# Second attention: the diffusion products as one stream over 25 row tiles' periods, and the last tile's normalization on VectorE

## The chip, the cores and the metric

The kernel runs on one core of a Trainium2 chip. The core has five engines that each work through their own list of instructions in order and wait for one another by semaphores: TensorE (PE; its weight loads are shown as PEld), VectorE (DVE), ScalarE (ACT), GpSimd (POOL) and SyncE (SP), which issues the DMAs here. The metric is the device time of one execution in microseconds (us); a time given for a kernel is the median of its runs.

## The reference, cut to what matters

A graph with 3327 nodes and 256 features passes through four layers. Each layer's output is added to its input and normalized. The change lies in the last layer, the fourth, which does two steps of this:

```
R = adj + I;  R = R / R.sum(-1, keepdims=True)
for n in range(2):
    A  = top_p_attention(Xa, W1, W2, W3)   # N x N, row by row, top-p = 0.9
    Xf = R @ Xf                            # diffusion
    Xa = A @ Xa                            # attention
    Z  = Z + Xf @ U1[n].T + Xa @ U2[n].T
h = X + Z
out = (h - mean) / sqrt(var + 1e-5) * ln_g + ln_b
x   = layernorm(x + out)
```

`top_p_attention` takes a softmax of a row's logits, keeps the largest probabilities until their sum reaches 0.9, and normalizes what is kept. The kernel computes the exponentials and finds the smallest kept value by a search; it divides by the kept sum at the end, after the product with the values.

## The kernel before, in words

The rows are cut into nt = 26 tiles of 128. The second attention (L1778 to L1840) is a loop `for i in range(-2, nt + 1)`; one pass of it is called a period here, with the number i. In period i several generators are stepped in turn, so that their instructions stand interleaved:

- `logits` (`scores`, L1141): the 832-column pieces of the logits of tile i + 2, two matmuls each (L1154), copied to `e` by ScalarE.
- `searches` (`search_long`, L1421): the search of tiles i, i + 1 and i + 2, in steps. ScalarE makes six passes over a row of 3328 (L1436, L1441, L1456, L1458, L1474, L1487), GpSimd does the one-column arithmetic between them (most at L1444), VectorE then selects candidates (L1503, L1353), ranks them (L1364, L1366), removes ties (L1532) and masks `e` (L1540; for the last tile in two halves at L1534).
- `values` (`attended`, L1318): tile i - 1. The masked `e` is transposed on TensorE in groups of four blocks (L1327), copied to `wt` by ScalarE (L1139 is the helper's line of these copies), and multiplied by the values G (L1341), 26 products.
- `spread` (`diffused`, L1302, and `aggregated`, L1288): a diffusion tile, 26 products of adjacency blocks with the features (L1296), each 128x128 by 128x256; every product shows as two records of TensorE. The adjacency comes in six loads of up to five blocks (L1294, three buffers), a stored sum `s` in another (L1309); GpSimd prepares `t` (L1306, L1310), and VectorE evacuates the accumulator into `xf` (L1315).
- `result` (`second`, L1583): the end of tile i - 2. VectorE combines value accumulator and `xf` (L1586) and takes statistics (L93, L94); GpSimd takes the power of the variance (`power`, L877, L878), standardizes (L1595), multiplies and adds (L1596, L1597); VectorE takes statistics again, GpSimd the power again and a bias (L1605); ScalarE does the second normalization (L1606), and SP stores the tile (L1608).

The diffusion tile of period i is i + 1 (DL = 1): period -1 does tile 0, period 0 tile 1, and so on to period 24 with tile 25. Periods 25 and 26 have no diffusion. At the end of each period what is left of the diffusion tile is finished (`both(spread)`).

The order of instructions on each engine is made by a scheduler that follows the program's order as priority and starts what is ready in its own estimate. ScalarE's passes and copies of this loop, marked `here` or `in_order`, keep the program's order. Value and diffusion accumulators come from the same three PSUM buffers (`acc`), `xf` has four buffers, `t` has two, which `second` shares.

After the loop the last `result` is run to its end, and `unresolved` (L1611) computes a flag for each tile whose search has to be repeated: a few small VectorE instructions, a one-column matmul (L1627), and a read by every engine (L1914) that decides whether a slow branch runs.

Of the kernel before, what the change touches and what calls it, by code (L numbers as in the profile page):

```python
# [9 lines left out]
F32 = mybir.dt.float32  # L10
# [3 lines left out]
ALU = mybir.AluOpType  # L14
# [4 lines left out]
P = 128  # L19
# [23 lines left out]
DL = 1  # L43
# [7 lines left out]
def gnn_kernel(ctx: ExitStack, tc: tile.TileContext, n: int, a: dict, out: bass.AP):  # L51
    nc = tc.nc
    nt = -(-n // P)
# [5 lines left out]
    small = ctx.enter_context(tc.tile_pool(name="small", bufs=4))  # L59
# [31 lines left out]
    def stats(mv, y, order=lambda x: x):  # L91
        st = small.tile([P, 6], F32, name="bnst")
        order(nc.vector.bn_stats(st, y))  # L93
        nc.vector.bn_aggr(mv, st)  # L94

    def standardize(dst, y, mean, rstd):
        nc.vector.tensor_scalar(dst, y, mean, rstd, op0=ALU.subtract, op1=ALU.mult)
# [79 lines left out]
    with tc.tile_pool(name="l1b", bufs=1) as wpool, tc.tile_pool(name="l1at", bufs=2) as l1at:  # L177
# [3 lines left out]
        with tc.tile_pool(name="l0", bufs=1) as pool, tc.tile_pool(name="l0w", bufs=2) as work, \  # L181
# [11 lines left out]
            for j0 in range(0, nh, J0):  # L193
                m = min(J0, nh - j0)
# [17 lines left out]
            for i in range(nh):  # L212
# [12 lines left out]
                for r in range(2):  # L225
                    it = 2 * i + r
# [13 lines left out]
        with tc.tile_pool(name="l1aw", bufs=1) as cwork, tc.tile_pool(name="l1c", bufs=2) as ch, \  # L240
# [103 lines left out]
            def power(rs, var):  # L344

                gps.tensor_scalar(rs, var, EPS, None, op0=ALU.add)
                gps.tensor_tensor(rs, rs, mhalf[:, :var.shape[1]], op=ALU.pow)
# [128 lines left out]
            shares = {}  # L476
# [264 lines left out]
            for k, (c, s) in enumerate(states):  # L741
                w = us[c].shape[2]
                m = tiles_of(c)
# [59 lines left out]
                if c and 9 <= s < 9 + tiles_of(c - 1):  # L803
                    rs, nb = plus[:2]
                    i = s - 9
                    x = X[:, starts[c - 1] // P + i, :]
# [37 lines left out]
            m = tiles_of(nch - 1)  # L844
            h = prods[k % 2]
# [4 lines left out]
            for i in range(m):  # L850
                it = starts[nch - 1] // P + i
# [16 lines left out]
    with tc.tile_pool(name="l3", bufs=1) as pool, tc.tile_pool(name="l3d", bufs=1, space=DRAM) as dram:  # L868
# [433 lines left out]
        def diffused(work, atp, psum, p, it, out, each=J3):  # L1302

            rd = rdeg[:, it:it + 1]
            t = work.tile([P, D], F32, name="t")
            nc.gpsimd.tensor_scalar(t, (Y if p else X)[:, it, :], rd, None, op0=ALU.mult)  # L1306
            if p:
                s = work.tile([P, D], F32, name="s")
                nc.sync.dma_start(s, sd[it])  # L1309
                nc.gpsimd.tensor_tensor(t, t, s, op=ALU.add)  # L1310
            for acc in aggregated(atp, psum, it, Y if p else X, each):
                if acc is None:
                    yield
            d = work.tile([P, D], F32, name="xf", bufs=DL + 3)
            nc.vector.scalar_tensor_tensor(d, acc, rd, t, op0=ALU.mult, op1=ALU.add)  # L1315
            out.append(d)
# [266 lines left out]
        def second(work, psum, it, acc, f, xf):  # L1583

            h = work.tile([P, D], F32, name="h")
            nc.vector.scalar_tensor_tensor(h, acc, f, xf, op0=ALU.mult, op1=ALU.add)  # L1586
            xb = work.tile([P, D], F32, name="t")
            nc.gpsimd.tensor_tensor(xb, X[:, it, :], b3, op=ALU.add)
            mv = small.tile([P, 2], F32, name="mv")
            stats(mv, h)  # L1590
            rs = small.tile([P, 1], F32, name="rs")
            yield
            with tc.issue_after(edge[0].ins) if edge[0] else nullcontext():
                power(rs, mv)
                nc.gpsimd.tensor_scalar(h, h, mv[:, 0:1], rs, op0=ALU.subtract, op1=ALU.mult)  # L1595
            nc.gpsimd.tensor_tensor(h, h, g3, op=ALU.mult)  # L1596
            nc.gpsimd.tensor_tensor(h, h, xb, op=ALU.add)  # L1597
            yield
            mv = small.tile([P, 2], F32, name="mv")
            stats(mv, h, here)  # L1600
            rs = small.tile([P, 1], F32, name="rs")
            power(rs, mv)
            yield
            nb = small.tile([P, 1], F32, name="nb")
            nc.gpsimd.tensor_scalar(nb, mv[:, 0:1], rs, -1.0, op0=ALU.mult, op1=ALU.mult)  # L1605
            here(nc.scalar.activation(h, h, AF.Identity, scale=rs, bias=nb))  # L1606
            m = min(P, n - it * P)
            nc.sync.dma_start(out[it * P:it * P + m, :], h[:m, :])  # L1608
            yield

        def unresolved(sm, psum, p):  # L1611


            tol = 4e-6
            tot, v, kept = tots[p], vs[p], kepts[p]
            a, f1, f2 = (sm.tile([P, nt], F32, name=x, bufs=1) for x in ("fa", "f1", "f2"))
            nc.vector.scalar_tensor_tensor(a, tot, -TOP_P, kept, op0=ALU.mult, op1=ALU.add)
            nc.vector.scalar_tensor_tensor(f1, tot, tol, a, op0=ALU.mult, op1=ALU.add)

            nc.vector.tensor_scalar(f1, f1, 0.0, None, op0=ALU.is_ge)  # L1620
            nc.vector.tensor_sub(a, a, v)
            nc.vector.scalar_tensor_tensor(f2, tot, -tol, a, op0=ALU.mult, op1=ALU.add)
            nc.vector.scalar_tensor_tensor(f1, f2, 0.0, f1, op0=ALU.is_lt, op1=ALU.mult)
            nc.vector.tensor_scalar(f1, f1, -1.0, 1.0, op0=ALU.mult, op1=ALU.add)
            nc.vector.tensor_mul(f1[:, nt - 1:], f1[:, nt - 1:], valid)
            pf = psum.tile([P, 4, P], F32, name="tp")[:1, 0, :nt]
            nc.tensor.matmul(pf, ones[:, 0:1], f1, start=True, stop=True)  # L1627
            fl = pool.tile([1, nt + 1], F32, name=f"fl{p}")
            nc.vector.tensor_copy(fl[:, :nt], pf)
            nc.vector.reduce_sum(fl[:, nt:], pf, axis=AX.X)  # L1630
            return fl

        def both(*parts):

            parts = list(parts)
            while parts:
                parts = [x for x in parts if next(x, parts) is not parts]

        with tc.tile_pool(name="l3w", bufs=2) as work, tc.tile_pool(name="l3s", bufs=4) as sm:
# [13 lines left out]
            with tc.tile_pool(name="l3p", bufs=2, space=PSUM) as psum, tc.tile_pool(name="l3a", bufs=1) as quads:  # L1653
# [62 lines left out]
                spread = spreading(1)  # L1716
# [61 lines left out]
            with tc.tile_pool(name="l3q", bufs=3, space=PSUM) as psum, tc.tile_pool(name="l3at", bufs=3) as atp, \  # L1778
                    tc.tile_pool(name="l3b", bufs=2) as lone:
                es, searches, xfs = {}, {}, []  # L1780
                result = iter(())
                for i in range(-2, nt + 1):
                    def search(t):
                        if 0 <= t < nt:
                            next(searches[t])

                    values, logits, spread = iter(()), iter(()), iter(())
                    if 0 < i:
                        values = attended(lone, psum, es[i - 1], G, 3, in_order(nc.scalar.copy))
                    if i + 2 < nt:  # L1790
                        logits = start(1, i + 2, es, searches, search_long)
                    more = range(len(xfs), min(nt, i + DL + 1))
                    spread = (x for j in more for x in diffused(lone, atp, psum, 1, j, xfs, 1))

                    def slot(products, looks, pair=False):


                        if pair:
                            next(logits, None)
                        for _ in range(products * len(more)):  # L1800
                            next(spread, None)
                        if pair:
                            next(logits, None)
                        next(values, None)
                        search(looks)

                    search(i)
                    slot(3, i + 1, True)
                    next(result, None)
                    search(i)  # L1810
                    search(i + 1)
                    search(i)
                    next(logits, None)
                    next(result, None)
                    for _ in range(3 * len(more)):
                        next(spread, None)
                    next(logits, None)
                    search(i + 2)
                    next(values, None)
                    search(i)  # L1820
                    next(result, None)
                    slot(3, i + 1, True)
                    slot(3, i + 1, True)
                    for _ in result:
                        pass
                    both(logits)
                    search(i)
                    slot(5, i + 2)
                    search(i + 1)
                    search(i)  # L1830
                    slot(5, i + 1)
                    slot(4, i + 1)
                    both(spread)
                    search(i)
                    if 0 < i:
                        f = normalizer(sm, kepts[1][:, i - 1:i], tots[1][:, i - 1:i])
                        result = second(lone, psum, i - 1, next(values), f, xfs[i - 1])
                both(result)
                edge[0] = None
                fl = unresolved(sm, psum, 1)  # L1840

            fi0 = pool.tile([1, nt + 1], I32, name="fi0")
            fi1 = pool.tile([1, nt + 1], I32, name="fi1")
# [139 lines left out]
```

## Time and profile before

| | |
|---|---|
| median of 3 runs | 3426.72 us (3426.38 to 3440.84) |
| the profiled execution's own time | 3433.03 us |
| its span, first to last instruction | 3431.1 us |
| busy share of the span | PE 92%, PEld 75%, DVE 78%, ACT 51%, POOL 33% |
| mean granted TensorE clock | 0.964 |
| second attention, from the first attention's flags to the end | 2566.6 to 3431.1 us |

The span is what the profiler saw of one execution; the time of that execution is 1.9 us longer. Times in the views count from the span's start. A busy TensorE is not TensorE at its peak, since matmuls overlap and their ends are modelled; the spacing of starts says more than a single duration. In a line of the timeline the bracket gives the idle time of the engine just before and the instruction that ended it.

### The profile page before, as it was taken

The numbers are of one execution on the slowest core, as the hardware profiler recorded it, in microseconds if no ns is written. First come the engines' busy times: TensorE is split into PE (matmuls) and PEld (weight loads), VectorE is DVE, ScalarE is ACT, GpSimd is POOL, SyncE is SP. The second block draws the span as 40 slices with busy tenths as digits, with TensorE's granted clock in tenths as the row PEclk, the third lists the DMA queues.
The fourth block names the chain that finished last, engine by engine and source line by source line (L and its number), as shares of the span: only waits on it lengthen the run. The fifth ranks groups of instructions, "written<-read, shape, count | busy, mean of one in ns | idle before, by whom it ended". The sixth has DMA issues, their size and how long they took to land. (4 is left out here: it accounts for less than half of the span.)

```text
span 3431.1 us, 50276 instructions
## 1 busy us (share of the span) xinstructions
PE 3140.4 (92%) x18301; PEld 2565.8 (75%) x18301; DVE 2686.5 (78%) x5895; ACT 1735.4 (51%) x2764; POOL 1127.6 (33%) x1332
## 2 busy tenths in 40 slices
PE   8999888898988776999989999999998999999996
PEld 5999657676675554888778888888885677777775
DVE  4655368999999997877578778778755898988886
ACT  1000456767767675111133333333337788888883
POOL 0000245666665654111400000000003566656563
PEclk9999999999999988999999999999998999999998
DMA  6775334334343322444322232232213122222220
GB/s 200 251 253 188 105 101 125 110 108 116 102 115 89 69 57 81 150 137 151 115 76 87 65 88 79 69 89 80 71 50 102 52 68 68 64 66 65 72 64 16
DMA packets 206264, 344.31 MB, mean 100 GB/s; under 512 B 22223, under 2 KB 129167, under 8 KB 205871
## 3 DMA queue, kind: packets, MB, share of 16 engines
q1 hardware_dynamic: 205998, 340.92, 33.2%
q8 instruction: 148, 2.42, 0.3%
q14 instruction: 118, 0.96, 0.1%
HBM read 304.65 MB, written 36.21 MB: 99 GB/s over the span
## 5 line engine op out<-in xcount | busy, mean ns | idle before, releaser
L330 POOL TENSOR_TENSOR h<-du,row 128x2048 f32<-128x2048 f32 (+1 forms) x110 | 465.5, 4232 | 344.9 <-DVE hc L330 248.6
L330 DVE TENSOR_TENSOR_SCAN h<-dA,carry,h 128x512 f32<-128x512 f32 (+1 forms) x384 | 449.0, 1220 | 18.2 <-ACT dA L337 18.1
L337 ACT ACTIVATE dA<-t,A_log 128x512 f32<-128x512 f32 (+1 forms) x448 | 292.5, 658 | 147.1 <-DVE h L330 145.5
L1296 PE MATMUL acc<-F,at 128*128 128x256 f32 x1352 | 354.3, 388 | 1.8 <-DMA at<-in_adjT 1.8
L1341 PE MATMUL acc<-G,wt 128*128 128x256 f32 x1352 | 336.6, 392 | 9.7 <-ACT wt L1139 9.3
L1341 PEld LDWEIGHTS acc<-G,wt 128*128 128x128 f32 x1352 | 250.1, 193 | 72.4 <-ACT wt L1139 42.2
L1079 PE MATMUL acc<-F,at 128*128 128x257 f32 x1352 | 303.4, 381 | 0.7 <-ACT r L1023 0.7
L389 PE MATMUL cb<-F,at 128*128 128x256 f32 x1196 | 295.5, 395 | 8.0 <-ACT hn L409 3.4
L1296 PEld LDWEIGHTS acc<-F,at 128*128 128x128 f32 x1352 | 239.3, 191 | 74.9 <-issue 46.6
L1146 POOL MEMSET e<- 128x1 f32 x52 | 4.9, 99 | 838.5 <-PE tp L891 769.5
L1079 PEld LDWEIGHTS acc<-F,at 128*128 128x128 f32 x1352 | 253.3, 190 | 36.2 <-issue 1.0
L680 PE MATMUL y<-ident,hc 128*128 128x128 f32 x1664 | 236.4, 296 | 46.2 <-DVE hc L330 46.1
L680 PEld LDWEIGHTS y<-ident,hc 128*128 128x128 f32 x1664 | 210.4, 154 | 87.4 <-DVE hc L330 62.6
L389 PEld LDWEIGHTS cb<-F,at 128*128 128x128 f32 x1196 | 229.8, 198 | 58.3 <-issue 19.4
L330 DVE TENSOR_TENSOR hc<-h,row 128x2048 f32<-128x2048 f32 (+2 forms) x114 | 243.2, 2135 | 11.3 <-PE y L680 4.3
L891 PE MATMUL acc<-X,at 128*128 128x128 f32 (+1 forms) x988 | 173.7, 287 | 6.0 <-issue 6.0
L1263 ACT COPY wt<-tp 128x512 f32<-128x512 f32 x156 | 90.8, 589 | 166.6 <-PE tp L891 153.2
L138 PE MATMUL acc<-t,cb 128*128 128x128 f32 (+1 forms) x1014 | 168.4, 275 | 0.0
L891 PEld LDWEIGHTS acc<-X,at 128*128 128x128 f32 x988 | 142.2, 193 | 29.9 <-issue 26.1
L891 PE MATMUL acc<-G,sw 128*128 128x128 f32 x936 | 155.5, 275 | 0.0
L891 DVE MAX8 cand<-e 128x8 f32<-128x128 f32 x676 | 139.8, 277 | 5.0 <-ACT e L1160 3.2
L1160 ACT COPY e<-sc 128x832 f32<-128x832 f32 x78 | 65.9, 845 | 149.2 <-PE sc L891 149.1
(414 smaller groups left out, 7263.0 us busy)
## 6 DMA issues: line engine op xcount, KB each, us to landing
at<-in_adjT SPq DMA_DIRECT2D x54, 832.0 KB, 4.5
at<-in_adjT SPq DMA_DIRECT2D x130, 320.0 KB, 3.0
row<-bc SPq DMA_DIRECT2D x80, 512.0 KB, 5.1
at<-in_adjT SPq DMA_DIRECT2D x52, 640.0 KB, 5.5
at<-in_adjT SPq DMA_DIRECT2D x52, 576.0 KB, 4.1
at<-in_adjT SPq DMA_DIRECT2D x72, 256.0 KB, 3.1
at<-mixed SPq DMA_DIRECT2D x72, 256.0 KB, 3.6
mixed<-cb SPq DMA_DIRECT2D x26, 640.0 KB, 4.2
```

The costliest lines, as they stand in the source:

```text
L138: mm = nc.tensor.matmul(acc, w[:, j, :], x, start=(y == 0 and k % 3 == 0 and k < 6), stop=(y == nh - 1 and k in (2, 6)))
L330: return lambda *x, **k: tc.keep_in_program_order(op(*x, **k))
L337: decays.append(op(*x, **k))
L389: ten.matmul(acc, at[:, j % JC, :], X0[:, j, :], start=(j == 0), stop=(j == nt - 1))
L680: x = ten.matmul(y[:, g * P:(g + 1) * P], h[:, g, i * P:(i + 1) * P], ident, is_transpose=True, start=(first and g == 0), stop=(last and g ...
L891: return lambda *x, **k: tc.keep_in_program_order(op(*x, **k))
L1079: nc.tensor.matmul(acc, at[:, j, :], F[:, j0 + j, :], start=(j0 + j == 0), stop=(j0 + j == nt - 1))
L1146: nc.gpsimd.memset(e[:, n:], NEG)
L1160: copy(halves[:, :, c0:c0 + ws[0]], pl[:, :, :ws[0]])
L1263: nc.scalar.copy(wts[-1], pt)
L1296: nc.tensor.matmul(acc, at[:, j, :], rhs[:, j0 + j, :], start=(j0 + j == 0), stop=(j0 + j == nt - 1))
L1341: tensor.matmul(acc, wt[:, j, :], rhs[:, j0 + j, :], start=(j0 + j == 0), stop=(j0 + j == nt - 1))
```

## The change: what it does

The generator `spread` is no longer made anew for each period. One stream runs over all 26 diffusion tiles, one product a step. Periods -1 and 0 take 26 steps each, as before; the remaining 624 are dealt out over periods 1 to 25, 24 or 25 each. Tile borders therefore slide through the periods. The evacuation of a tile is issued with the first product of the next one; the last one in period 26.

In `second` the last tile takes another way: both standardizations, the product with g3 and the sum with the bias are done on VectorE (`standardize`, L96), and only the power stays on GpSimd; the result is stored from there. The call of `unresolved` moves ahead of the last `result`.

```diff
@@ second
             rs = small.tile([P, 1], F32, name="rs")
+            if it == nt - 1:
+                for k in range(2):
+                    power(rs, mv)
+                    standardize(h, h, mv[:, 0:1], rs)
+                    if k == 0:
+                        nc.vector.tensor_tensor(h, h, g3, op=ALU.mult)
+                        nc.vector.tensor_tensor(h, h, xb, op=ALU.add)
+                        mv = small.tile([P, 2], F32, name="mv")
+                        stats(mv, h)
+                        rs = small.tile([P, 1], F32, name="rs")
+                m = min(P, n - it * P)
+                nc.sync.dma_start(out[it * P:it * P + m, :], h[:m, :])
+                return
             yield
@@ second attention
                 result = iter(())
+                spread = (x for j in range(nt) for x in diffused(lone, atp, psum, 1, j, xfs, 1))
+                later = (nt - 2) * nt
+                shares = [later * (k + 1) // (nt - 1) - later * k // (nt - 1) for k in range(nt - 1)]
                 for i in range(-2, nt + 1):
...
-                    values, logits, spread = iter(()), iter(()), iter(())
+                    values, logits = iter(()), iter(())
...
-                    more = range(len(xfs), min(nt, i + DL + 1))
-                    spread = (x for j in more for x in diffused(lone, atp, psum, 1, j, xfs, 1))
+                    share = iter(range(shares[i - 1] if 0 < i < nt else nt if -2 < i < 1 else 0))
+
+                    def diffuse(products):
+                        for _ in range(products):
+                            if next(share, None) is not None:
+                                next(spread, None)
...
-                        for _ in range(products * len(more)):
-                            next(spread, None)
+                        diffuse(products)
...
-                    for _ in range(3 * len(more)):
-                        next(spread, None)
+                    diffuse(3)
...
-                    both(spread)
+                    diffuse(nt)
                     search(i)
+                    if i == nt:
+                        for _ in spread:
+                            pass
...
+                fl = unresolved(sm, psum, 1)
                 both(result)
                 edge[0] = None
-                fl = unresolved(sm, psum, 1)
```

## The prediction

> **What bounds the kernel now.** I read the page first, then the stretches of the second attention (2566 to 3431 us), then its waits, then the timelines of TensorE, VectorE and GpSimd over the last 100 us. The page's chain of waits is of no use here: it stops at the last normalization, `ACT h L1606`. The page has PE at 92% overall, and that average hides two regimes.
>
> The stretches (columns: stretch, length, then busy us and instructions of PE, PEld, DVE, ACT, POOL, granted clock, DMA share, GB/s):
>
> ```profile
> 2719.00:2749.00 30.00, 27.63 (x134) 20.74 (x133) 26.87 (x79) 24.77 (x25) 18.67 (x37) 1.00 0.20 59
> 3055.00:3086.00 31.00, 30.81 (x150) 22.99 (x149) 27.62 (x83) 26.27 (x26) 18.87 (x37) 1.00 0.23 66
> 3358.00:3388.00 30.00, 22.53 (x108) 18.84 (x106) 26.37 (x79) 10.84 (x14) 12.36 (x29) 0.89 0.02 7
> 3388.00:3408.00 20.00, 16.16 (x67) 13.20 (x68) 15.05 (x46) 3.83 (x9) 4.57 (x8) 0.83 0.02 7
> ```
>
> From about 2780 to 3366 TensorE has no gap: L1606, once a period, starts at 3301.28 and 3331.87, a period of 30.6 us. In period 25 (3368 to 3399), without diffusion, TensorE has gaps and VectorE has none. The waits of 2780 to 3366 say the same: TensorE waits for almost nothing, VectorE waits for TensorE in each period.
>
> ```profile
> DVE h L1586 <- PE acc L1341: 25.6, 18, 1.5
> PE acc L1341 <- ACT wt L1139: 3.5, 18, 0.3
> ```
>
> TensorE's timeline, one normal group and then period 25 and 26 (start, length, what, in brackets the idle time before it and who ended it):
>
> ```profile
> 3335.20 1.46 PE L1296 MATMUL acc<-F,at 128*128 128x256 f32 x6
> 3336.49 0.60 PE L1327 MATMUL tp<-ident,e 128*128 128x128 f32 x4
> ...
> 3373.28 2.79 PE L1327 MATMUL tp<-ident,e 128*128 128x128 f32 x12 [4.73 <-DVE e L1540]
> ...
> 3388.86 7.57 PE L1341 MATMUL acc<-G,wt 128*128 128x256 f32 x20 [3.05 <-ACT wt L1139]
> 3399.05 1.06 PE L1327 MATMUL tp<-ident,e 128*128 128x128 f32 x8 [2.62 <-DVE e L1534]
> ```
>
> Three products (two records each) take 3336.49 - 3335.20 = 1.29 us, so 0.43 us each. In period 25 TensorE is ready early and waits for the searches. VectorE's path to them has one wait:
>
> ```profile
> 3362.70 0.16 DVE L1490 RECIPROCAL s<-s 128x1 f32<-128x1 f32 x1 [2.79 <-POOL s L1444]
> ```
>
> and from there to 3400.7, where the last search ends, it is busy without a pause. What sets 3362.70: POOL's `s` follows L1458 on ScalarE (3354.92), whose place in ScalarE's order is behind a copy (3354.44) of the transposes that TensorE did at 3353.80. So up to 3353.80 TensorE sets the end; from there it is ScalarE, GpSimd, VectorE; from 3399 TensorE again with the last values; then the tail:
>
> ```profile
> 3415.90 0.22 POOL L877 TENSOR_SCALAR rs<-mv 128x1 f32<-128x1 f32 x1 [8.06 <-DVE mv L94]
> 3416.20 0.56 POOL L878 TENSOR_TENSOR rs<-rs,mhalf 128x1 f32<-128x1 f32 x1
> 3416.86 1.25 POOL L1595 TENSOR_SCALAR h<-h,mv,rs 128x256 f32<-128x256 f32 x1
> 3418.19 0.72 POOL L1596 TENSOR_TENSOR h<-h,ln_g 128x256 f32<-128x256 f32 x1
> 3418.99 0.72 POOL L1597 TENSOR_TENSOR h<-h,t 128x256 f32<-128x256 f32 x1
> 3421.76 0.60 ACT L1606 ACTIVATE h<-h,nb,rs 128x256 f32<-128x256 f32 x1 [11.09 <-POOL nb L1605]
> ```
>
> The output's DMA is issued at 3422.39; 8.7 us follow to the end of the span.
>
> **What the Trainium skill says.** "Perfetto Trace Analysis", Optimization Strategy: where the most-contended engine changes over time, "performance may be improved by interleaving those regimes". The trace has such regimes. "TensorE: Matmul & The Clock Gate", What's actually happening: after an idle window of about 3.4 us the array runs at half clock until about 3.4 us of work have passed. The trace agrees: after 4.73 us idle the twelve transposes took 0.23 us each, after 2.62 us idle eight took 0.13. "GPSIMD Engine Reference", 3.1 Elementwise — side-by-side cycle accounting: GpSimd needs more cycles per element than VectorE. Here an add of 128x256 takes 0.72 us on POOL (L1597) and 0.42 on DVE (L1093).
>
> **The change part by part.** I counted instructions in the order in which both kernels are built.
>
> *Products moved.* Both do 676. Up to the transposes that release L1458 in period 24 both have done 610 value products, 614 transposes and all 208 logits; diffusion products are 662 before and 638 after. From period 6 on the difference grows by exactly one per period. 24 x 0.43 = 10.3 us that TensorE gets there earlier, if it stays busy throughout. Nothing else of the period is near its limit: from the period's last two transposes (3340.46) through L1487 and VectorE's chain the next e is masked 30.5 us later, and TensorE needs it some 2.5 us after the same place one period on, so a period of 30.17 leaves VectorE about 2 us.
>
> *The opening.* Period 2 carries fewer products than before (at the first eight transposes of period 3 the count is 104 against 115), because the fifth tile's accumulator now takes over the fourth's and waits for its evacuation. TensorE idles there anyway: it waits 2.66 us at 2698.85 for a search, and again 2.37 at 2731.05 and 2.32 at 2761.69. The displaced products are caught up in periods 3 to 5, where the last two waits (4.7 us) take them in: from 2700.6 to the same transposes in period 6 the old order took 98.3 us, with 5.0 of waits; the new one has 2.3 us more work and no reason for these two waits, so about 2.7 us less, which is the six products' 2.6. Net 0 beyond the count. Bounds: -0.8 (more idle removed) to +4.7 (both waits stay).
>
> *Evacuation L1315.* Its place on VectorE now slides through the period instead of standing beside L1540: 0.48 us as before. Behind it, when it waits, stand the search's steps. By the order, a tile's last product comes 0.5 to 3 us ahead of L1315 everywhere I followed it (second tile of the slide: product ends 3.1 us after the last value product, VectorE gets there at 3.8). 0 us; if it waits, 2 us a period are absorbed. The loads of the adjacency move with the stream on SP, the loads of `s` still stand more than a tile ahead, and GpSimd's sum with them stays behind the normalization: 0.
>
> *VectorE's order in period 24.* L1490, which waits for POOL, stands one step of the ranking earlier: a match-replace (3359.47 to 3359.91) that ran inside the wait now runs after it: +0.4 us on the path to the last e.
>
> *Period 25.* TensorE now has 20 diffusion products there, 8.6 us at full clock, beside 26 value products (0.45 each, 11.8) and 26 transposes (0.107 each, 2.8): 23.2 us. In the old kernel's times, all of it 10.3 earlier: its e comes at 3373.1, 0.9 later for the reorderings (L1490, L1315), and it has to be through at 3399. That leaves 2 us, of which the copies behind L1606 on ScalarE and the half clock after its 3 us wait (1.6 us lost after the 2.66 us wait at 2698.85, 3.0 at 3388.86) take some: 0 to 1.5 us late, I take 0.5. If this cover were missing the 8.6 us would be on the path.
>
> *Tail.* After the first pow (3416.76) VectorE does L97 0.41 (row of the first layer), product and sum 0.45 each with the step between them, statistics 0.45 and 0.18, then POOL's two (0.30 and 0.57) and L97 again 0.41, with 0.1 at each change of engine: issue at 3420.35 in place of 3422.39, -2.0 us. The flags stand in the same places of VectorE's order, between the statistics: 0. L1914's reading of them on SP stays behind the last DMA: 0.
>
> Sum: -10.3 + 0 + 0.4 + 0.5 - 2.0 = -11.4 us. The profiled span of 3431.1 would be 3419.7. The profiled execution took 3433.03, the median of the timed runs is 3426.72; I take the difference over to the median: 3415.3 us, 0.33% faster. 0.5% (17.1 us) is about what a measurement of this kernel can tell from no change, so this forecast lies within it.
>
> **Rivals.**
>
> *The gain is given back (14%).* The opening keeps its two waits (+4.7) or period 25 runs at half clock and delays the last tile by 3 us. For it: the PEclk of 0.89 and 0.83 in the last stretches, and the search still gates period 3. Against: TensorE's added work there closes the gaps that slow it. Time: 3415.3 + 3 to 7.7, so 3418.5 to 3423.
>
> *More is gained (7%).* The opening's waits go and nothing replaces them, and TensorE enters period 26 earlier than the search allows now: -11.4 - 4.7 - 1 = -17, so 3409 to 3410. Against: VectorE's chain in period 25 has no gap to give.
>
> *VectorE becomes the bound (5%), slower.* L1315 in the middle of the search waits for the diffusion tile's last product, and the whole search with it, in the nineteen or so periods in which it stands there. A stall up to about 2 us is absorbed, each us more costs 19 us; from 2.6 us on the gain is gone. At 3.8 us: -11.4 + 1.8 x 19 = +23, 3450 us. For it: VectorE is busy 27.6 of 31 us. Against: the order keeps the last product ahead of it.
>
> *The change doesn't do what it says* is excluded by the order: 19 to 20 products do move behind period 24.
>
> **How the numbers follow.** The main case has 74% and its own range 3412 to 3418.5. With the first two rivals' near ends 3411 to 3421.5 holds eight in ten. Below 3409.6 lies half a per cent faster: 6%; above 3443.9 slower: 5%; the rest, 89%, is within.
>
> **What would show it.** Right: L1606 30.17 us apart in the middle; TensorE without gaps from period 4 to 24; period 25 with L1296 in it and its wait for L1540 about 3 us; the last DMA 4.3 us (now 6.5) after the first L877 of the tail. Wrong: L1315 with idle time "<-PE acc"; waits of 2 us or more at the starts of periods 4 and 5; the first transposes of period 26 waiting not for L1534 but coming late behind L1341.

## The result, and the profile after

The changed kernel takes 3416.46 us (median of 7 runs) beside 3432.26 us of the kernel before (median of 7) on the same chip. One of its seven runs took 4558.13 us at a mean granted clock of 0.649 instead of 0.964 to 0.969, and the ratio leaves that run out: 0.9952 (95% interval 0.9943 to 0.9962), 16.5 us or 0.48% faster. That lies within the half per cent that the forecast named, and the 3416.46 lies near its 3415.3. The nearness is luck. The 3415.3 was built on 3426.72, the median of three runs; with more runs the kernel before stands at 3432.26. The *difference* was forecast as 11.4 us, and it is larger: 16.5 by the timed runs, 20.1 between the two profiled spans (3431.1 and 3411.0).

Of those 20.1 us, 2.3 lie ahead of the second normalization of tile 0, which stands at 2689.52 before and at 2687.22 after; over all kernels below it scatters from 2681 to 2691, with the stream or without. So I measure in the traces from there to the last L1586 (the last tile's value accumulator is read), and from that to the end of the span:

| | before | after | difference | forecast |
|---|---|---|---|---|
| tile 0 to tile 5 (five periods) | 152.7 | 151.6 | -1.1 | -2.8 |
| tile 5 to tile 21 (sixteen periods) | 489.7 | 475.0 | -14.7 | -6.9 |
| tile 21 to tile 24 (three periods) | 76.0 | 76.7 | +0.7 | +0.3 |
| tile 24 to the last L1586 | 6.8 | 6.1 | -0.7 | in the line above |
| last L1586 to the end | 16.5 | 14.5 | -2.0 | -2.0 |

The rows start and end at second normalizations (L1606, in the changed kernel L1619). The forecast's column deals its 24 products out to the rows, six to seven to the first and sixteen to the second, and has the 0.9 us of the reorderings in the third. The middle row holds the surprise: its regular periods are 29.52 us where the forecast had 30.17, against 30.59 before.

Three stretches of the changed kernel (columns as in the prediction); the second reaches from period 24 into 25, the third from 25 into 26:

```profile
3047.00:3077.00 30.00, 30.00 (x148) 22.82 (x147) 26.96 (x79) 24.82 (x24) 18.90 (x37) 1.00 0.22 62
3340.00:3370.00 30.00, 25.45 (x119) 20.82 (x118) 25.70 (x79) 10.35 (x13) 15.23 (x28) 0.94 0.21 62
3370.00:3390.00 20.00, 19.33 (x100) 16.12 (x99) 15.64 (x45) 3.83 (x8) 4.99 (x8) 1.00 0.02 7
```

TensorE still has no gap in the middle. Period 25 is now filled with products and runs at full clock but for its first microseconds (taken up below, where the prediction is gone through). The waits from 2780 to 3350, VectorE's and TensorE's:

```profile
DVE h L1586 <- PE acc L1341: 9.9, 15, 1.7
```

```profile
PE acc L1296 <- DVE top L1364: 0.9, 1, 0.9
PE acc L1296 <- DMA at<-in_adjT: 0.9, 1, 0.9
```

VectorE's wait for TensorE fell from 25.6 to 9.9 us, L1315 is not in its list, and the products (L1296) have two new waits of 0.9 us. TensorE's timeline at the start of period 25 and at its end:

```profile
3355.34 0.63 PE L1327 MATMUL tp<-ident,e 128*128 128x128 f32 x4 [4.55 <-DVE e L1540]
3355.80 0.82 PE L1296 MATMUL acc<-F,at 128*128 128x256 f32 x2
...
3357.06 3.07 PE L1341 MATMUL acc<-G,wt 128*128 128x256 f32 x8
...
3381.15 1.25 PE L1327 MATMUL tp<-ident,e 128*128 128x128 f32 x10
```

The transposes of period 26 no longer wait for L1534: its first half ends at 3380.69, TensorE comes at 3381.15, 0.5 us late. That is one of the signs that the prediction listed for being wrong, of the size that its own sum allowed. The tail, on VectorE and on SP's queue:

```profile
3398.70 0.41 DVE L97 TENSOR_SCALAR h<-h,mv,rs 128x256 f32<-128x256 f32 x1 [0.87 <-POOL rs L878]
...
3401.79 0.41 DVE L97 TENSOR_SCALAR h<-h,mv,rs 128x256 f32<-128x256 f32 x1 [1.07 <-POOL rs L878]
```

```profile
3402.23 0.29 SPq L1603 DMA_DIRECT2D out<-h  x1
```

GpSimd's first L877 of the tail is at 3397.81, so the store is issued 4.4 us after it, against 6.5 before.

**Where the surplus is.** The surplus is what was gained beyond the forecast. TensorE's order changed along with the count. TensorE's work in a period falls into seven groups, called slots here: each ends with the value products of one group of transposes. In four of them a piece of the logits is made first (L1154). Before, such a slot mostly stood as logits, one product, four transposes, two products, four value products; after, three in four stand as logits, four transposes, three products, four value products. One slot of each, before and after (each product and each value product is two records):

```profile
3107.44 0.97 PE L1154 MATMUL sc<-kT,q 64*128 64x416 f32 x4
3108.34 0.70 PE L1296 MATMUL acc<-F,at 128*128 128x256 f32 x2
3108.88 0.60 PE L1327 MATMUL tp<-ident,e 128*128 128x128 f32 x4
3109.31 1.03 PE L1296 MATMUL acc<-F,at 128*128 128x256 f32 x4
3110.21 1.99 PE L1341 MATMUL acc<-G,wt 128*128 128x256 f32 x8
```

```profile
3122.24 0.97 PE L1154 MATMUL sc<-kT,q 64*128 64x416 f32 x4
3123.14 0.66 PE L1327 MATMUL tp<-ident,e 128*128 128x128 f32 x4
3123.64 1.46 PE L1296 MATMUL acc<-F,at 128*128 128x256 f32 x6
3124.94 1.89 PE L1341 MATMUL acc<-G,wt 128*128 128x256 f32 x8
3126.76 0.97 PE L1154 MATMUL sc<-kT,q 64*128 64x416 f32 x4
```

The next logits of the kernel before start at 3112.13: 4.69 us for the old slot, 4.52 for the new one, with the same three products in it. Two differences make up most of it. A product right after logits takes 0.54 us to the next start instead of 0.43, transposes there 0.49 to 0.50 instead of 0.44. And the value products wait at their first weight load for ScalarE's copy of the transposes (0.58 us on ScalarE): in the old slot, with two products (0.87 us) between transposes and values, the copy comes just too late; in the new one, with three (1.30 us), it doesn't. Over 2780 to 3350 the weight loads' waits for the copy (us in total, times, longest) are, before and after:

```profile
PEld acc L1341 <- ACT wt L1139: 30.8, 107, 0.7
```

```profile
PEld acc L1341 <- ACT wt L1139: 19.0, 81, 0.6
```

Start to start, the seven slots of a regular period took 5.02, 4.63, 4.69, 4.54, 4.40, 4.40 and 2.90 us before (from 3097.79 on), and 5.15, 4.52, 4.51, 4.42, 3.97, 4.41 and 2.55 after (from 3146.61 on). The three slots with transposes first give 0.41 of the 1.07 us. The first slot keeps one product ahead, but now has three more behind its transposes, so it holds four products instead of three for only 0.13 us more: its 0.19 us of open wait for the copy is gone. The fifth and the last slot each have a product less and give 0.43 and 0.35.

The theory to test: of the 1.07 us a period, 0.43 is the product less and the rest is this order. Its rival: the one stream itself saves it, since no tile has to be finished at a period's end.

### The profile page after: what moved, and what is told of

Same layout as the page of the kernel before. It is cut to its first block, busy times and chain, and to the rows that moved or that the text cites. A ratio compares the mean times of both kernels' runs of the same rounds, so it can differ in the third digit from the quotient of the medians.

```text
span 3411.0 us, 50267 instructions
## 1 busy us (share of the span) xinstructions
PE 3129.6 (92%) x18301; PEld 2561.4 (75%) x18301; DVE 2687.8 (79%) x5899; ACT 1729.9 (51%) x2763; POOL 1132.1 (33%) x1328
## 5 line engine op out<-in xcount | busy, mean ns | idle before, releaser
L1296 PE MATMUL acc<-F,at 128*128 128x256 f32 x1352 | 343.9, 383 | 3.0 <-DMA at<-in_adjT 2.1
L1296 PEld LDWEIGHTS acc<-F,at 128*128 128x128 f32 x1352 | 240.7, 190 | 53.2 <-issue 21.5
L389 PEld LDWEIGHTS cb<-F,at 128*128 128x128 f32 x1196 | 229.4, 198 | 58.5 <-issue 19.6
L330 DVE TENSOR_TENSOR hc<-h,row 128x2048 f32<-128x2048 f32 (+2 forms) x114 | 242.9, 2133 | 11.4 <-PE y L680 4.3
```

Source lines behind the costliest of these rows:

```text
L330: return lambda *x, **k: tc.keep_in_program_order(op(*x, **k))
L389: ten.matmul(acc, at[:, j % JC, :], X0[:, j, :], start=(j == 0), stop=(j == nt - 1))
L1296: nc.tensor.matmul(acc, at[:, j, :], rhs[:, j0 + j, :], start=(j0 + j == 0), stop=(j0 + j == nt - 1))
```

## The experiments

Lengths in the table are from each kernel's trace: the regular middle period, and the change against before from tile 0's second normalization to the last L1586 and from there to the end. The last column is the timed gain against before (one less the ratio, times the median of before, 95% interval). The rounds ran on four chips, on which the kernel before had medians of 3434.09 (e1 to e4), 3431.87 (e5 to e8), 3426.55 (e9, e10) and 3428.75 (e11, e12); each kernel is compared with before on its own chip. The +1.1 and +0.2 of e2 and e6, whose middle periods are those of before, show how well a length to the last L1586 repeats.

| kernel | products in a period | order in a slot with logits | period | to L1586 | to the end | timed gain |
|---|---|---|---|---|---|---|
| before | 26 | one product ahead | 30.59 | 0 | 0 | |
| after | 25 | three of four: transposes first | 29.52 | -15.8 | -2.0 | 16.5 (13.0 to 19.6) |
| e1 | 25 | as after | 29.52 | -16.0 | 0.0 | 14.4 (10.3 to 18.5) |
| e2 | 26 | as before | 30.59 | +1.1 | -2.0 | 3.4 (0.3 to 6.2) |
| e3 | 26 | transposes first | 29.52 | -17.6 | +0.1 | 16.8 (11.0 to 22.7) |
| e4 | 25 | one product ahead | 30.44 | -3.2 | -2.0 | 11.3 (6.9 to 15.8) |
| e5 | 25 | transposes first | 29.15 | -26.1 | -2.0 | 23.3 (18.5 to 27.8) |
| e6 | 26, one stream | one product ahead | 30.59 | +0.2 | -2.0 | 2.1 (-1.0 to 5.1) |
| e7 | as e5 | as e5 | 29.15 | -26.2 | -2.8 | 28.5 (23.7 to 33.3) |
| e8 | as e5 | as e5 | 29.15 and up | -22.2 | -4.5 | 23.7 (18.9 to 28.1) |
| e9 | as after | as after | 29.52 | -15.6 | -2.0 | 19.5 (14.0 to 25.0) |
| e10 | as e5 | as e5 | 29.15 | -26.0 | -3.6 | 33.6 (27.8 to 39.1) |
| e11 | as after | as after | 29.52 | -16.4 | -1.9 | 19.5 (14.7 to 24.3) |
| e12 | as e5 | as e5 | 29.15 | -26.4 | -3.4 | 34.6 (29.5 to 40.1) |

### e1 and e2: the stream and the tail, each alone

e1 is the changed kernel without the branch for the last tile and with the flags back behind it; e2 is the kernel before with these two edits alone.

```diff
# e1: changed kernel
-            if it == nt - 1:
-                for k in range(2):
...
-                return
...
-                fl = unresolved(sm, psum, 1)
                 both(result)
                 edge[0] = None
+                fl = unresolved(sm, psum, 1)
```

> The stream over 25 periods without the new tail: the last tile's normalization and the place of the flags are those of the kernel before. The prediction's sum without its tail gives -9.4 us against before. The theory after the result (a middle period of 29.5 us instead of 30.6, so more than one product's 0.43 us) gives -14.4 by the timed runs and about -18 between profiled spans, L1586 of the last tile some 18 us earlier. If the tail were worth more than 2 us, it would be less than -14.

> The kernel before with the new tail alone (last tile normalized on VectorE, flags ahead of it), TensorE's order untouched. The prediction's tail step: -2.0 us, the last store issued 4.3 us after the tail's first L877 in place of 6.5, middle periods 30.6 us. If the missing 5 to 8 us of gain came from the tail: -7 or more.

The tail is worth 2.0 us and the stream 16.0 in the trace (14.4 timed), and in the trace the two add up to the whole change. The surplus is in e1: in the stream or in the order that came with it. e1 has the same 29.52 us periods, and the same two long ones (30.62 and 30.75).

### e3: the order alone, without the stream

```diff
# e3: kernel before; attended() calls between() after turn()
+                between()
                 wt = wts.pop(0)
...
-                        for _ in range(products * len(more)):
-                            next(spread, None)
+                        due.extend(range(products * len(more)))     # between() takes these, spend() the rest
                         if pair:
                             next(logits, None)
                         next(values, None)       # transposes, due products, value products
+                        spend()
...
```

> The kernel before, still 26 products a period and none in period 25, but a slot's products are put behind its transposes in the program, so that TensorE's order in the slots with logits is logits, 4 transposes, 3 products, 4 value products, in place of logits, 1 product, 4 transposes, 2 products, 4 value products. Order theory: a slot falls by about 0.145 us (0.538 + 0.436 + 0.870 + 1.913 in place of 0.492 + 1.30 + 1.82), four slots a period, 0.6 us over 18 periods: middle period 30.0 us, -10 to -13 us against before, and the waits of L1341's weight loads for L1139 shrink. Rival theory (the surplus comes from the one stream, whose tile borders slide and whose period has no end at which a tile must be finished): middle period 30.6, 0 +- 1 us.

With the same 26 products a period the middle period is 29.52 us, and the kernel gains 16.8 us: as much as the whole change, with neither its stream nor its tail. TensorE's slots in e3:

```profile
3094.48 0.97 PE L1154 MATMUL sc<-kT,q 64*128 64x416 f32 x4
3095.38 0.66 PE L1327 MATMUL tp<-ident,e 128*128 128x128 f32 x4
3095.87 1.46 PE L1296 MATMUL acc<-F,at 128*128 128x256 f32 x6
3097.17 1.89 PE L1342 MATMUL acc<-G,wt 128*128 128x256 f32 x8
3098.99 0.97 PE L1154 MATMUL sc<-kT,q 64*128 64x416 f32 x4
```

The four slots with logits of one period take 4.51, 4.51, 4.51 and 4.42 us here, in place of 5.02, 4.63, 4.69 and 4.54. That is 0.93 of the 1.07 us; the other 0.14 are two slots without logits, where five products after the transposes in place of two save 0.07 each. I had expected 0.6 a period: the first of the four slots, where 0.19 us of the wait for the copy stands open, was not in that sum. The weight loads' wait for the copy is nearly gone over 2780 to 3340:

```profile
PEld acc L1342 <- ACT wt L1139: 0.9, 3, 0.4
```

### e4: the stream with the old order

```diff
# e4: changed kernel, in slots with logits of periods 6 to 23
+                        with tc.issue_after(piece[0].ins):      # piece: last matmul of the logits
+                            diffuse(1)
...
+                with tc.issue_after(ahead_of[0].ins):           # ahead_of: that product
                     for j in range(m):
                         tensor.transpose(pt[:, j, :], e[:, (j0 + j) * P:(j0 + j + 1) * P], ident)
```

> The changed kernel with the same 25 or 24 products a period, but in periods 6 to 23 one product is forced between logits and transposes, as it stood before: logits, 1 product, 4 transposes, 2 products, values. Order theory: 0.54 us a period over 18 periods are lost again, +9.7 us against the changed kernel, so about -7 us against before; middle period 30.1 us. Rival theory (order does not matter, the stream does): no change against the changed kernel, -16 us against before, middle period 29.5.

With 25 products in the old order the period is 30.44 us: the product less is worth 0.15, not 0.43. In the first slot the values read:

```profile
3095.83 1.99 PE L1347 MATMUL acc<-G,wt 128*128 128x256 f32 x8 [0.32 <-ACT wt L1139]
```

The product was taken out of the last slot of the period, where only one is left between two transposes and their values, and there the weight load now waits for the copy:

```profile
3091.54 0.73 PEld L1347 LDWEIGHTS acc<-G,wt 128*128 128x128 f32 x4 [0.43 <-ACT wt L1139]
```

That slot falls from 2.90 us to 2.77 only, 0.13 in place of 0.43. In the first slot the open wait for the copy grew from 0.19 to 0.32, which costs 0.13. The two slots of five products, which stand as two, transposes, three instead of three, transposes, two, give 0.07 each. These make the 0.15: a product that covers a copy is worth little when it goes. The timed loss against the changed kernel is 5 us, the trace's 12.6, the expected 9.7, and the trace's gain of 5.2 over before lies below the timed interval: timed runs and profile agree on the direction and leave its size open.

### e5: both together

```diff
# e5: changed kernel, as e3
-                        diffuse(products)
+                        ahead = 0
+                        diffuse(ahead)
+                        due.extend(range(products - ahead))
...
```

> The changed kernel (25 or 24 products a period, new tail) with the transposes ahead of a slot's products everywhere, as in e3. In e3 26 products gave a middle period of 29.52 us, the same as 25 in the changed kernel. Order theory: that is chance, TensorE's groups add up to 29.52 in both (0.43 for one product against the changed kernel's remaining single products ahead of transposes), so 25 products in this order take 29.1 us: 18 x 0.43 = 7.7 us less than the changed kernel, about -23 us against before. Rival theory: 29.52 is a floor that another engine's chain sets, VectorE's search above all; then the period stays 29.5 and TensorE gets waits of 0.4 us a period: no gain over the changed kernel, -16 us against before.

That e3 with 26 and the changed kernel with 25 products both show 29.52 us could have been another engine's floor. It is chance: with 25 products in the new order the period falls to 29.15, 0.37 less for one product. VectorE is not the bound yet at 29.15. So dealing the products out is worth 8.5 us (e5 against e3, to L1586) once the order lets it. The changed kernel itself stands 1.8 us behind e3 to L1586, products dealt out and all: a quarter of its slots keep the old order, and three of its periods are long.

### e6: the stream without the dealing

```diff
# e6: changed kernel
-                shares = [later * (k + 1) // (nt - 1) - later * k // (nt - 1) for k in range(nt - 1)]
+                shares = [nt] * (nt - 2) + [0]
```

> The changed kernel with its one stream, sliding evacuation included, but with 26 products in each of periods 1 to 24 and none in period 25; TensorE's order is then the old one (logits, 1 product, 4 transposes, 2 products, values). Order theory: middle period 30.6 us, only the tail's 2 us are left: -2 to -3 us against before. Rival theory (the stream itself saves the surplus): middle period 30.0 or less, -12 us or more.

One stream with sliding evacuation, 26 products in each of 24 periods: period 30.59, nothing gained but the tail's 2.0 us. The rival falls: 26 products in the old order take what they took, as one stream or not. e3 (the order alone gives 1.07 us a period), e4 (the product less in the old order gives 0.15) and e6 (the stream alone gives 0) together show that the order carries the surplus. How the 1.07 us of the changed kernel divide between product and order has no one answer, since the worth of a product depends on the order: 0.15 in the old one, 0.37 in the new. Why the scheduler puts the transposes first when a period holds 25 products, and one product first when it holds 26, stays open; it follows its own estimate of what is ready.

### e7: the last store in two

```diff
# e7: e5
-                nc.sync.dma_start(out[it * P:it * P + m, :], h[:m, :])
+                k = m // 16 * 16
+                for r in (slice(0, k), slice(k, m)):
+                    if r.stop > r.start:
+                        nc.sync.dma_start(out[it * P + r.start:it * P + r.stop, :], h[r, :])
```

> e5 with the last store of 127 rows issued as two, 112 rows and 15 rows. In the profiles so far the span ends 8.7 us after that store's issue, and the one queue row moves some 25 GB/s meanwhile[...]. If the store runs on one engine because of its 127 rows, the span ends some 4.5 us after the issue: -4 us against e5. Rival: the 8.7 us are fixed cost of the end of the program: 0 or slower by one more issue (0.3 us).

Mostly a miss. The span ends 8.0 us after the first of the two stores is issued, against 8.8 in the changed kernel; the DMA view gives their time from issue to landing (last column, us):

```profile
out<-h SPq DMA_DIRECT2D x1, 112.0 KB, 3.3
out<-h SPq DMA_DIRECT2D x1, 15.0 KB, 4.2
```

Bytes do move faster at first, 84 GB/s from 3391.5 to 3393.0 against 28 in the changed kernel from 3402.2 to 3406.0. But the second store takes SP 2.21 us to issue (0.47 to 1.6 in the other kernels that have it, 0.3 for a first one), from 3391.13 on, and lands at 3395.3; another 3.4 us follow to the end at 3398.7. Against e5 the stretch from the last L1586 to the end is 0.8 us shorter here, and 1.4 to 2.5 us shorter in e8, e10 and e12, which have the split and other edits. Why the second issue is slow, and what the last 3.4 us are, stays open.

### e8, e9, e11: the two long periods

The theory for the changed kernel's periods of 30.65 and 30.70 us: loads of the adjacency come late. SP's queue and, in the same place, TensorE:

```profile
2879.91 0.33 SPq L1294 DMA_DIRECT2D at<-in_adjT  x1
2892.20 0.33 SPq L1309 DMA_DIRECT2D s<-sd  x1
2892.63 0.85 SPq L1294 DMA_DIRECT2D at<-in_adjT  x2
```

```profile
2895.74 0.70 PE L1296 MATMUL acc<-F,at 128*128 128x256 f32 x2 [0.87 <-DMA at<-in_adjT]
```

SP waits for GpSimd's L1310 (ends at 2892.2), which reads the buffer that the next `s` goes to, and two loads of the adjacency stand behind it. This wait was there before too (168 us in sixteen times over 2780 to 3350), but in the kernel before, whose tiles end with a period, no product waited for a load in that stretch. The profile puts the other long period's wait down to VectorE's L1364; in e1 both read "DMA at<-in_adjT", so I take both for the load.

> e7 with the sum of input and bias in a tile of its own name instead of t, so that GpSimd's L1588 no longer waits for the evacuation L1315 in a buffer that it shares with the diffusion tiles. In the changed kernel two middle periods are 1.1 us longer: TensorE waits 0.9 us there for a load of the adjacency issued late on SP behind a load of s. Theory: GpSimd's wait for L1315 (9.6 us in four times) delays that load; without it both waits go, -2 us against e7. Rival: the load is late for another reason, 0.

```diff
# e8: e7
-            xb = work.tile([P, D], F32, name="t")
+            xb = work.tile([P, D], F32, name="xb")
```

e8's two waits for the adjacency are gone, but its periods vary from 29.15 to 31.0 and it loses 4.0 us against e7 up to the last L1586: from 2780 to 3340 TensorE now waits for the search's end (L1541, 2.8 us) and the copies (2.5 us), and VectorE waits for GpSimd's `level` (10.4 us in eight times from 2960 to 3200). I take it that GpSimd's work now comes in another order against the search; this was not followed further.

> The changed kernel with three buffers in place of two for s, the stored sum that a diffusion tile adds, so that its load is issued one tile earlier and SP no longer waits some 10 us for GpSimd's L1310 with loads of the adjacency queued behind; TensorE's order is untouched. Theory: the two middle periods of 30.65 and 30.70 us and the one of 29.86 fall to 29.52, and with them the two waits of 0.9 us of L1296: -2.6 us against the changed kernel. Rival: the loads are late by TensorE's own release of their buffers (L1294 waits 273 us for L1296 in the same stretch): nothing changes.

```diff
# e9: changed kernel
-                s = work.tile([P, D], F32, name="s")
+                s = work.tile([P, D], F32, name="s", bufs=3)
```

No effect in the trace: the long periods are 30.95 and 30.78. The scheduler used the third buffer to issue the load a tile earlier, and SP waits as before:

```profile
SPq L1309 <- POOL t L1310: 147.4, 15, 11.9
```

This neither supports nor refutes the theory, since the wait that it blames was not removed.

> The changed kernel with the load of s put behind the same tile's third load of the adjacency in SP's order, and the sum with it (L1310) to the middle of the tile, so that the buffer that the load takes was read long before and SP does not wait for GpSimd with loads of the adjacency queued behind; two buffers as in the changed kernel, TensorE's order untouched. (e9's third buffer only let the scheduler issue the load a tile earlier: SP still waited 147 us.) Theory: SP's wait for L1310 goes, so do the two waits of L1296 for the adjacency, and the two long middle periods fall to 29.5 us: -2.3 us against the changed kernel, seen in the trace rather than in the timed ratio. Rival: the load behind them is late anyway: no change, or new waits of VectorE for a later t.

```diff
# e11: changed kernel, diffused(): the load and the sum after half of the products
+                if p and done == (13 if each == 1 else 2):
+                    s = work.tile([P, D], F32, name="s")
+                    with tc.issue_after(loaded[0].ins):        # loaded: the tile's last load so far
+                        nc.sync.dma_start(s, sd[it])
+                    nc.gpsimd.tensor_tensor(t, t, s, op=ALU.add)
```

SP's wait for GpSimd's sum (L1315 here) is gone from its list, both long periods are 29.52, and no product waits for a load. This settles the cause of these two. The third long period of the changed kernel, 29.86 us, has another: it is 30.61 here. By the traces, GpSimd waits in that place for VectorE's evacuation, since the sum of input and bias goes to a buffer `t` that the diffusion tile still uses. ScalarE's next pass comes late after it, then the copy behind this pass, then TensorE's values. GpSimd's wait in the changed kernel, and TensorE's here, where GpSimd's is 2.24 us:

```profile
3110.82 0.73 POOL L1588 TENSOR_TENSOR t<-X,ln_b 128x256 f32<-128x256 f32 x1 [1.51 <-DVE xf L1315]
```

```profile
3118.50 1.13 PE L1346 MATMUL acc<-G,wt 128*128 128x256 f32 x4 [0.90 <-ACT wt L1139]
```

One more period rose to 29.82 us. Net 0.6 us gained in the trace, which is less than such a length repeats to; the timed interval does not tell it from the changed kernel either.

### e10 and e12: what beats both

> e7 (stream, transposes first everywhere, split store) with the third buffer for s of e9. Theory: middle periods 29.15 us throughout, the 2.8 us of the three long ones gone; -29 to -31 us against before, about -13 against the changed kernel. Rival as in e9: the same as e7, -28 us.

> e7 (stream, transposes first everywhere, split store) with the load of s held as in e11. Theory: middle periods 29.15 us throughout, 2.6 us less than e7 between the first tile's and the last tile's end, about -31 us against before. Rival as in e11: as e7, -28 us.

e10 is e7 with e9's third buffer, e12 is e7 with e11's edit. e10 keeps its two long periods (30.47 and 30.37). e12 has neither, but two of 30.0 and 29.9; to the last L1586 it is 0.2 us ahead of e7, which is nothing. Both run at 3395 to 3396 us: 0.9902 (0.9886 to 0.9919) and 0.9899 (0.9883 to 0.9914) of the kernel before, twice the gain of the change. That the third buffer or the held load helps is not shown, since the intervals of e7, e10 and e12 overlap; the order and the split store are what they share. In the traces, with the tail, they gain 29.6 and 29.8 us (e7: 29.0), at the lower end of the timed intervals.

## Why the prediction was right or wrong

- **Products moved, -10.3.** This step had its size wrong. It took 24 products off, each at its spacing in the old order (0.43 us), and used the order of both kernels for counting only. That three of the four slots with logits now have their transposes ahead of the products, and that a product moved to the first slot, was priced at nothing, without a reason. In the middle sixteen periods the step gives -6.9 us; measured are -14.7. Regular periods that are 1.07 us shorter would make -17.1 there; the three long ones give 2.7 back (next points), and the rest is one period of 30.87 us in the kernel before. The order alone is worth those 1.07 us in e3, and the product alone 0.15 in e4, so even the -6.9 is not the worth of the products by themselves.
- **Nothing else near its limit.** Right as far as tested: e5 goes to 29.15 without VectorE as the bound.
- **The opening, 0.** The two waits at the starts of periods 4 and 5 went, as written (in the changed kernel 0.3 and 0.2 us are left, on ScalarE's copy). From tile 0 to tile 5 the gain is 1.1 us where the count gives 2.8, so by this reckoning the opening cost 1.7 us, inside its bounds of -0.8 to +4.7.
- **L1315 and the loads, 0.** VectorE never waited at L1315: right. That "the loads of `s` still stand more than a tile ahead" was true and missed the point: the load is early, and it is its own wait for L1310 that holds what stands behind it on SP. The sliding border met that twice: 30.65 and 30.70 us in place of 29.52, 2.3 us. The step also looked only at what L1315 waits for and at what stands behind it on VectorE. GpSimd waits for L1315 too (L1588), and by the traces that made the third long period, 29.86.
- **L1490, +0.4, and period 25, +0.5.** With the products of these periods +0.3, measured 0.0 from tile 21 to the last L1586. The wait of L1490 for POOL is 3.2 us (2.8 before). Period 25 is 0.5 us late, and the first value products after the 4.55 us wait ran slow (3.07 us for eight records, 1.97 later): the granted clock was 1.00 up to 3356, about half from there to 3359.4, then 1.00 again. What the prediction took from the Trainium skill ("TensorE: Matmul & The Clock Gate", What's actually happening), that an idle window of about 3.4 us leads to half clock, its trace bears out only in part. It named the waits of 4.73 us (half clock) and 2.62 us (full clock), but after idle times of 2.66 us (2698.85) and 3.05 us (3388.86) the granted clock was 0.50 too, so here the length of one wait does not decide it. L1540's wait is 4.6 us, not 3, since TensorE comes earlier than forecast.
- **Tail, -2.0.** -2.0 (-1.9 to -2.0) in each kernel that has it and stores once, 4.4 us from L877 to the store where the forecast had 4.3.
- **The rivals.** "More is gained" (-17, 7%) has the right size by luck: the opening, which was its reason, did not bring it. VectorE as the bound did not come. "The gain is given back" happened in part (1.7 us in the opening) and was outweighed.
- **The level.** The forecast took the difference over to a median of three runs, 3426.72; seven runs on the same chip gave 3432.26. The level was 5.5 us too low and the difference 5.1 us too small, so that the two errors cancel near 3416. That is luck.

## What to carry to other kernels

When a scheduler decides the order, compare the order of groups as well as the counts, and price each group by what stands before and after it. Between transposes and the products that use them stands a copy, and other work has to cover it: here two products (0.87 us) did not quite cover a copy of 0.58 us, and three (1.30 us) did. In a slot of the kernel before, the transposes started at 3104.24, the copy ran from 3104.88 to 3105.46, and the weight load that needed it, free 0.21 us earlier, followed at 3105.52. A product taken out where it covered such a copy gives little (e4). An engine that is busy throughout can still lose time inside its groups: before, TensorE was busy 238.5 of 240 us from 2960 to 3200, and e3 does the same work of a period in 3.5% less time. And a load issued early can still block a queue, by its own wait for a buffer.

## What the runs showed of the hardware that I had not expected

- A busy TensorE hid 1.07 us in 30.59. The Trainium skill ("Trainium Kernel Development and Optimization", Best Practices) says to judge TensorE's distance from its limit by the share of peak arithmetic reached and by the busy share of the weight loads, not by the matmuls'. The trace agrees for the weight loads: from 2960 to 3200 the matmuls read 238.50 us before and 240.00 in e3, which does more work in that time, and the weight loads 177.86 and 188.27.
- After the logits' matmuls (64 rows of contraction) the next group starts slower: a product takes 0.54 us to the next start instead of 0.43, four transposes 0.49 instead of 0.44. The weight loads there are listed as waiting for "issue" (0.6 us); the reason stays open.
- The profile put a 0.9 us wait for a load down to L1364 of VectorE in one run and to the load in another, in the same place of the program (changed kernel and e1).
